# When the row additions, the expert work and the last chunk's row numbers are issued in a graph and expert layer

## The chip, the cores and the metric

The kernel runs on one core of a Trainium2 chip. The metric is the device time of one execution in microseconds. A time is the median of several runs; a profile comes from one execution. The engines are called PE (matrix), PEld (its weight loads), DVE (vector), ACT (scalar), POOL (general purpose, here only the sender of indirect transfers) and SP (here only a sender of transfers). Each takes its own instructions in their written order and waits on semaphores for the others.

## The reference, cut to what matters

There are 6250 nodes with 256 features and 100,000 edges, sorted by destination. The layer is a mean over neighbours with a linear map, and then a mixture of eight experts of which each node uses two:

```python
x = x + gnn(layernorm(x), edge_index)     # segment_sum(h[src], dst) / degree, then [h, agg] @ W.T + b
xn = layernorm(layernorm(x)) * gamma + beta
logits = xn @ Wr + br
top_vals, top_idx = top_k(logits, 2)
w = softmax(top_vals)
for e in range(8):
    h = gelu(xn @ W1[e] + b1[e])          # 256 -> 512
    y_e = h @ W2[e] + b2[e]               # 512 -> 256
    y = y + y_e * w_full[..., e, None]
out = x + y
```

All of it is computed in float32.

## The kernel before, in words

**Edges.** The 100,000 edges are padded to 784 *edge tiles* of 128. Fourteen tiles (`C`) make a *window*, and there are 56 windows (`W`). First the kernel forms `z_d`, the neighbour product of every node, and `u_d`, the node's own product. Then it takes one edge tile after another. `gather` (L553) is an indirect transfer on POOL of 128 rows of `z_d` into one of 28 buffers `xg` (`XG`), issued 28 tiles ahead of its use. `add_edges` (L570) multiplies these rows by a matrix of zeros and ones `hot` (made on DVE, L564), so that edges with one destination add up in the PSUM tile `pS`. When the 14 tiles of a window are through, `window_done` plans what follows: `shared_row` (L576, DVE) adds the row that two windows share, `keep_sums` (L580, ACT) copies the sums, `share_row` sends the row on to the next window by way of memory, and `window_x1` (L605 to L608) divides by the degree and adds the node's own product, which `load_u` (L597) has fetched. For the last window `load_u` is an indirect transfer on POOL (L599).

**Routing.** Four windows make a *chunk*, 14 in all. After a chunk's last window `window_done` plans the routing by counts of tiles: variances, roots, norms, the router's logits, the ranking (`route`), `exps`, `weigh`, `choices`, `count_tokens`, then for each of four windows `one_hot_slots` (L644, L645) and `sort_tokens` (L652 on PE, L655 on ACT), which sorts the tokens by expert into `xs`. `share_runs`, `place_rest`, `place_runs` and `tile_experts` work out on DVE where each run of tokens goes. `copy_runs` (L786, ACT) copies the runs of one expert into the slots `xe`, in eight calls of four copies each. `find_rows` (L756 on PE, L760 to L769 on DVE) gives each token the row number of its two results. `start_experts` releases the chunk's expert work. The class `Steps` holds the counts of tiles for the ordinary chunks and `LastSteps` those for the last chunk, whose routing comes behind the last edge.

**Expert work.** `expert_stages` gives 16 *tasks* for a chunk: eight `hidden` (L811 on PE, L816 Gelu on ACT) and eight `result` (L824 on PE; after every second one L828 on DVE adds the bias and L830 on SP stores 256 rows of `y`). The PSUM tile `py` has one buffer, so the next pair of results waits for L828. Chunks are joined in three *batches* of 6, 5 and 3 chunks. After a batch's last chunk `more_stages` does tiles of 128 tokens that overflowed their slots (7, 5 and 3 of them, three tasks each: L854, L858; L863, L866; L872, L876, L879).

**Additions.** When all expert work of a batch is planned, `sum_rows` starts the *additions*, one for each window: `gather_rows` loads the window's rows from `x1_d` (L908, SP) and its two result rows by two indirect transfers on POOL (L912), into the `xg` buffers that the edges no longer need. `add_rows` adds them with two L919 on DVE and `store` writes 128 rows of the output (L898, SP; the last window by an indirect transfer on POOL, L900). Additions start only where fewer than 28 edge tiles are left.

**What sets the order.** The order is written out by hand. The loop over edge tiles calls `after(t)` once for each tile `t`, and further with counts up to the end. `after` first issues what was planned with `at` for this `t`. Then it adds `pace` to an allowance, issues tasks from the list `tasks` until the allowance is spent, and calls `sum_rows`. `clock` is the planner's own estimate of time, by which an addition counts as due 10 us after its gather:

```python
        while adds and (adds[0][0] <= clock or not (sums or tasks)):
            adds.pop(0)[1]()
```

In this text *step* `t` is one call of `after`; the last edge tile is step 783.

Of the kernel before, what the change touches and what calls it, by code (L numbers as in the profile page):

```python
# [19 lines left out]
C = 14  # L20
TB = 4
UB = 2
CW = 4
# [7 lines left out]
def gnn_ffn_kernel(ctx: ExitStack, tc: tile.TileContext, x, x_cols, src, dst, dst_next, gw, gw_t, gb, gb_cols, gamma, beta,  # L31
# [39 lines left out]
    W = src.shape[1]  # L71
# [833 lines left out]
    def gather_rows(K, j, V):  # L905
        g = K.first + j
        V.o = spare()
        nc.sync.dma_start(V.o, x1_d[g * P:(g + 1) * P, :])  # L908
        G, i = K.group, j
        V.y2 = [spare() for _ in range(2)]  # L910
        for r in range(2):
            nc.gpsimd.indirect_dma_start(  # L912
                out=V.y2[r], out_offset=None, in_=K.batch.y[:, :],
                in_offset=bass.IndirectOffsetOnAxis(ap=G.rows[:, r, i:i + 1], axis=0))

    def add_rows(K, j, V):
        G, i = K.group, j
        for r in range(2):
            nc.vector.scalar_tensor_tensor(V.o, V.y2[r], G.w2[:, r, i:i + 1], V.o, op0=ALU.mult, op1=ALU.add)  # L919
        store(K, j, V.o)  # L920
# [4 lines left out]
    tasks, later, Ks, sums, adds = [], {}, [], [], []  # L925
    slots, w1_sb, w2_sb, xe = None, None, None, None
    now, spent, clock, due, spares = None, 0.0, 0.0, 0.0, 0
    class Steps:

        x1, var, roots, norms, route, exps, weigh, choices, count = 2, 5, 7, 9, 11, 14, 15, 16, 19  # L930
        hot, sort = (22, 24, 26, 28), (26, 28, 30, 32)
        runs, rest, place, tiles, copied, rows, pace, start = 30, 33, 36, 39, 40, 46, 1.5, 54

    class LastSteps:

        x1, var, roots, norms, route, exps, weigh, choices, count = 2, 4, 5, 6, 7, 8, 9, 10, 12
        hot, sort = (13, 14, 17, 18), (15, 16, 19, 20)
        runs, rest, place, tiles, copied, rows, pace, start = 15, 16, 19, 24, 21, 28, 1, 25

    def at(t, f, *args):  # L940
        later.setdefault(max(t, now), []).append(lambda: f(*args))
# [44 lines left out]
    def sum_rows():  # L986

        nonlocal due
        while adds and (adds[0][0] <= clock or not (sums or tasks)):
            adds.pop(0)[1]()  # L990
        left = W * C - 1 - now
        while sums and not sums[0][0].batch.left and clock >= due and left < XG:
            if 0 < left < XG and spares + 3 > XG - left:
                return
            K, j = sums.pop(0)
            V = Group()
            gather_rows(K, j, V)
            adds.append((clock + 10.0, lambda K=K, j=j, V=V: add_rows(K, j, V)))
            while len(adds) > XG // 3 - 1:
                adds.pop(0)[1]()  # L1000
            due = max(due, clock - 6.0) + (4.0 if left > 0 else 2.4)

    def after(t):
        nonlocal now, spent, clock
        now = t
        while later.get(t):
            later[t].pop(0)()
        later.pop(t, None)
        clock += 0.6 if t < W * C else 0.3 if tasks else 1.2

        pace = 0.72 if t < W * C else 1.2 if len(Ks) < W // CW else 2.0
        spent = min(spent + pace, pace) if tasks else 0.0
        while tasks and spent > 0:
            us, f, _ = tasks.pop(0)
            spent -= us
            clock += us
            f()
        sum_rows()
# [13 lines left out]
    for index in range(W // CW):  # L1032
# [10 lines left out]
        for g in range(K.first, K.first + CW):  # L1043
            if g > 0:
                V = V_next
            for c in range(C):
                t = g * C + c
                add_edges(V, c)
                if c == 0:
                    hot_tiles(V, HC)  # L1050
                if c == HC and g + 1 < W:
                    V_next = new_window(g + 1, V)
                if t + XG < len(edge_tiles):
                    gather(*edge_tiles[t + XG])
                for to, what in loads[:1]:
                    loads.pop(0)
                    nc.sync.dma_start(to, what)
                if u_tasks and t % 2 == 0:
                    u_tasks.pop(0)()
                    if not u_tasks:  # L1060
                        u_pools.close()
                        slots = fast_pools.enter_context(tc.tile_pool(name="slots", bufs=2))
                        xe = slots.tile([P, KD, SC], F32, name="xe", bufs=1)
                        for n in range(4):
                            at(t + 3 + 5 * n, clear_slots, n)
                        w1_sb, w2_sb, parts = weights(slots)
                        for n, (to, what) in enumerate(parts):
                            at(t + 2 + 2 * n, nc.scalar.dma_start, to, what)
                if c == HC + 5:
                    load_u(V)  # L1070
                if c == C - 1:
                    window_done(V, G, K, t)
                after(t)
    t = W * C
    while later or tasks or sums or adds:
        after(t)
        t += 1
# [149 lines left out]
```

## Time and profile before

| | |
|---|---|
| time, median of 3 runs | 1244.61 us (1242.8 to 1246.04) |
| profiled execution, its own time | 1243.91 us |
| its span, first to last instruction | 1242.0 us |
| PE busy | 1024.7 us (83%) |
| PEld busy | 870.2 us (70%) |
| DVE busy | 705.5 us (57%) |
| ACT busy | 454.6 us (37%) |
| POOL busy | 859.5 us (69%) |
| granted PE clock, mean | 0.924 of full |

The span is what the lines of the profile add up to; the execution's own time is 1.9 us longer, and the median of the runs is 0.7 us above that. Busy shares are means over very different stages: up to about 1055 us the edges run, and after it the last chunk is routed, its experts run, and nearly all the additions are made. POOL's busy time leaves out the pause of about 0.3 us between two of its indirect transfers, so that an engine that sends without a break shows as three quarters busy.

### The profile page before, as it was taken

What the parts mean: (1) busy time and instruction counts of PE and PEld (TensorE: products, weight loads), DVE (VectorE), ACT (ScalarE), POOL (GpSimd) and SP (SyncE); (2) the same over time, 40 slices, a digit from 0 to 9 for tenths busy, and PEclk for the clock granted to TensorE, in tenths of its full rate; (3) what the DMA queues carried; (4) which work ended last, traced back from release to release, by engine and by line L of the source; (5) the groups of instructions that cost most, each with busy time, mean ns of one, the idle gap of its engine ahead of it and who ended that gap; (6) DMA issues with size and microseconds to landing.
All of it is one profiled execution on the core that took longest, in us unless ns stands there. A gap on an engine that the chain in (4) does not pass through costs nothing. (4 is left out here: it accounts for less than half of the span.)

```text
span 1242.0 us, 18821 instructions
## 1 busy us (share of the span) xinstructions
PE 1024.7 (83%) x5236; PEld 870.2 (70%) x5236; DVE 705.5 (57%) x2436; ACT 454.6 (37%) x1264; POOL 859.5 (69%) x907
## 2 busy tenths in 40 slices
PE   7898837897979798897979999997979999675920
PEld 6676625786868687786857898886868788565710
DVE  5766657474646566464547556563655664483442
ACT  2400003534444344434443554435444544334200
POOL 0057777777777777777777777777777777775554
PEclk9999878898989899998999999998989999787965
DMA  9989895554555555454555555555555555665664
GB/s 335 359 277 310 251 368 151 137 154 137 156 142 148 152 144 155 136 160 130 154 141 161 140 154 153 153 153 144 148 146 151 151 154 149 198 197 165 192 182 131
DMA packets 139187, 221.02 MB, mean 178 GB/s; under 512 B 23108, under 2 KB 106255, under 8 KB 138950
## 3 DMA queue, kind: packets, MB, share of 16 engines
q0 software_dynamic: 43104, 120.94, 36.4%
q1 hardware_dynamic: 87638, 89.37, 21.7%
q10 hardware_dynamic: 8336, 9.45, 2.3%
q8 instruction: 44, 0.72, 0.2%
q14 instruction: 65, 0.53, 0.1%
HBM read 166.69 MB, written 53.02 MB: 177 GB/s over the span
## 5 line engine op out<-in xcount | busy, mean ns | idle before, releaser
L553 POOL DMA_INDIRECT xg<-z_d,src_i x784 | 747.7, 954 | 306.3 <-issue 115.5
L570 PE MATMUL pS<-xg,hot 128*128 128x265 f32 x1568 | 418.5, 398 | 20.1 <-issue 7.3
L570 PEld LDWEIGHTS pS<-xg,hot 128*128 128x128 f32 x1568 | 295.8, 196 | 78.7 <-issue 14.9
L811 PE MATMUL ph<-xe,w_sb 128*128 128x128 f32 x1792 | 237.3, 290 | 68.2 <-ACT xe L786 68.2
L811 PEld LDWEIGHTS ph<-xe,w_sb 128*128 128x128 f32 x1792 | 233.7, 205 | 79.5 <-ACT xe L786 73.1
L824 PE MATMUL py<-w_sb,hid 128*128 128x256 f32 x896 | 219.0, 390 | 13.5 <-DVE rows L828 13.5
L816 ACT ACTIVATE hid<-ph,b_sb 128x128 f32<-128x128 f32 x448 | 128.1, 369 | 243.5 <-PE ph L811 243.2
L824 PEld LDWEIGHTS py<-w_sb,hid 128*128 128x128 f32 x896 | 172.0, 195 | 42.4 <-ACT xe L786 13.0
L786 ACT ACTIVATE xe<-xs x448 | 139.3, 311 | 135.7 <-DVE rows L828 39.9
L912 POOL DMA_INDIRECT xg<-y_d,rows_i x112 | 108.5, 969 | 61.4 <-issue 19.8
L564 DVE TENSOR_TENSOR hot<-cols,rel 128x896 f32<-128x896 f32 x112 | 121.2, 1082 | 36.3 <-PE pS L570 33.1
L576 DVE TENSOR_TENSOR pS<-pS,row 1x265 f32<-1x265 f32 x55 | 23.5, 427 | 141.1 <-PE pS L570 130.1
L655 ACT ACTIVATE xs<-pm,beta_sb,gamma_sb 128x256 f32<-128x256 f32 x112 | 57.2, 560 | 75.5 <-PE pm L652 75.3
L828 DVE TENSOR_TENSOR rows<-py,b_sb 128x512 f32<-128x512 f32 x56 | 38.4, 685 | 79.7 <-PE py L824 77.1
L919 DVE SCALAR_TENSOR_TENSOR xg<-xg,w,xg 128x256 f32<-128x256 f32 x112 | 52.8, 483 | 37.6 <-DMA xg<-y_d,rows_i 34.9
L580 ACT ACTIVATE sums<-pS 128x265 f32<-128x265 f32 x56 | 21.7, 388 | 125.7 <-DVE pS L576 50.9
L255 PE MATMUL ph<-gc,x_t 128*128 128x264 f32 (+1 forms) x200 | 56.1, 404 | 11.8 <-DVE u_t L372 7.3
L652 PE MATMUL pm<-to,xn 128*128 128x256 f32 x224 | 57.6, 380 | 2.7 <-DVE to L645 2.7
L255 PEld LDWEIGHTS ph<-gc,x_t 128*128 128x128 f32 x200 | 37.4, 194 | 23.6 <-issue 7.1
L255 PE MATMUL pm<-gc,x_t 128*128 128x264 f32 (+1 forms) x192 | 53.1, 400 | 0.0
L816 ACT ACT_TABLE_LOAD x24 | 30.8, 1283 | 57.1 <-PE ph L811 56.9
L652 PEld LDWEIGHTS pm<-to,xn 128*128 128x128 f32 x224 | 42.4, 190 | 9.7 <-issue 3.0
(189 smaller groups left out, 817.9 us busy)
## 6 DMA issues: line engine op xcount, KB each, us to landing
y_d<-rows SPq DMA_DIRECT2D x56, 256.0 KB
xg<-z_d,src_i POOLq DMA_INDIRECT x784, 2.9
w_sb<-w_dram ACTq DMA_DIRECT2D x16, 512.0 KB
sums_d<-sums SPq DMA_DIRECT2D x55, 132.5 KB
x<-u_d SPq DMA_DIRECT2D x55, 132.0 KB
x_d<-x SPq DMA_DIRECT2D x56, 128.0 KB
xg<-x_d SPq DMA_DIRECT2D x56, 128.0 KB
out_dram<-xg SPq DMA_DIRECT2D x55, 128.0 KB
```

Source lines behind the costliest of these rows:

```text
L255: nc.tensor.matmul(pz, x_t[:, t, k, :], gc[:, h * KD + k, :n], start=(k == 0), stop=(k == KD - 1))
L553: nc.gpsimd.indirect_dma_start(out=xg[(g * C + c) % XG][:, :DZ], out_offset=None, in_=z_d[:, :], in_offset=bass.IndirectOffsetOnAxis(ap=sr ...
L564: nc.vector.tensor_tensor(hot, col[:, None, :].to_broadcast([P, HC, P]), V.rel[:, c:c + HC, None].to_broadcast([P, HC, P]), op=ALU.is_equal)
L570: nc.tensor.matmul(V.pS, V.hot[c // HC][:, c % HC, :], xg[(V.g * C + c) % XG], start=(c == 0), stop=(c == C - 1))
L652: nc.tensor.matmul(px[:, k, :], G.xn[i][:, k * P:(k + 1) * P], G.one_hot[i], start=True, stop=True)
L655: nc.scalar.activation(xs[:, at:at + 2 * P], px[:, k, :], AF.Identity, bias=beta_sb[:, k:k + 1], scale=gamma_sb[:, k:k + 1])
L786: nc.scalar.activation(xe[:, :, bass.ds(to_at, CAP)], src[:, :, bass.ds(src_at, CAP)], AF.Copy)
L811: nc.tensor.matmul(ph[:, i, a * SH:(a + 1) * SH], w1_sb[:, U.e + a, k, c * P:(c + 1) * P], xe[:, k, at:at + SH], start=(k == 0), stop=(k = ...
L816: nc.scalar.activation(U.hid[:, c, a * SH:(a + 1) * SH], ph[:, i, a * SH:(a + 1) * SH], AF.Gelu, bias=b1_sb[:, U.e + a, c:c + 1])
L824: nc.tensor.matmul(U.py[:, h, :], U.hid[:, c, h * P:(h + 1) * P], w2_sb[:, U.e + h, c, :], start=(c == 0), stop=(c == KH - 1))
L912: nc.gpsimd.indirect_dma_start(out=V.y2[r], out_offset=None, in_=K.batch.y[:, :], in_offset=bass.IndirectOffsetOnAxis(ap=G.rows[:, r, i:i ...
L919: nc.vector.scalar_tensor_tensor(V.o, V.y2[r], G.w2[:, r, i:i + 1], V.o, op0=ALU.mult, op1=ALU.add)
```

## The change

Four things change, all of them in when something is issued; no instruction is added or taken away.

- `start` of the ordinary chunks goes from 54 to 60 steps behind the chunk's last edge tile. The copies of a chunk are issued at steps 40 to 50.
- For the last chunk `rows` goes from 28 to 22 and `start` from 25 to 29. Its copies are issued at 21 to 28.
- `sum_rows` issues due additions only once the last edge tile has been issued. (Its second loop, which issues the oldest addition when nine are open, stays.)
- In the last 50 edge tiles `pace` is 0.4 in place of 0.72.

```diff
     class Steps:
 ...
-        runs, rest, place, tiles, copied, rows, pace, start = 30, 33, 36, 39, 40, 46, 1.5, 54
+        runs, rest, place, tiles, copied, rows, pace, start = 30, 33, 36, 39, 40, 46, 1.5, 60
 
     class LastSteps:
 ...
-        runs, rest, place, tiles, copied, rows, pace, start = 15, 16, 19, 24, 21, 28, 1, 25
+        runs, rest, place, tiles, copied, rows, pace, start = 15, 16, 19, 24, 21, 22, 1, 29
 ...
     def sum_rows():
 
         nonlocal due
-        while adds and (adds[0][0] <= clock or not (sums or tasks)):
+        while adds and now >= W * C and (adds[0][0] <= clock or not (sums or tasks)):
             adds.pop(0)[1]()
 ...
-        pace = 0.72 if t < W * C else 1.2 if len(Ks) < W // CW else 2.0
+        pace = 0.4 if W * C - 50 <= t < W * C else 0.72 if t < W * C else 1.2 if len(Ks) < W // CW else 2.0
```

## The prediction

> **What bounds the kernel now.** I read the costliest groups first, then the waits, then the timeline engine by engine from 1040 us on. The chain that ended last is of no use here: it goes back only to 1234 us. The waits of POOL (engine, line, who was waited for: total us, times, longest us):
>
> ```profile
> POOL xg L553 <- issue: 115.5, 379, 0.3
> POOL xg L553 <- PE pS L570: 71.0, 233, 0.3
> ```
>
> No edge gather waits longer than a pause of 0.3 us, whoever is named, after the one long wait at the start. From 149.2 to 1054.9 us POOL sends one every 1.2526 us (1054.90 - 1053.65 in the timeline). So the edge stage is as long as POOL's queue, and PE's 68.2 us of waiting for the copies (L811 on L786) cost nothing while edges run. The change can move only what lies behind 1056 us, some 186 us of 1242. The timeline there (start us, length us, engine, line; in brackets the idle time before and its releaser):
>
> ```profile
> 1054.90 0.95 POOL L553 DMA_INDIRECT xg<-z_d,src_i  x1 [0.30 <-issue]
> 1056.16 0.94 POOL L912 DMA_INDIRECT xg<-y_d,rows_i  x1 [0.30 <-issue]
> ...
> 1059.43 0.48 DVE L919 SCALAR_TENSOR_TENSOR xg<-xg,w,xg 128x256 f32<-128x256 f32 x1 [12.08 <-DMA xg<-y_d,rows_i]
> ...
> 1067.29 3.75 PE L824 MATMUL py<-w_sb,hid 128*128 128x256 f32 x8 [12.26 <-DVE rows L828]
> ...
> 1078.26 0.95 POOL L599 DMA_INDIRECT x<-u_d,tail_i  x1 [0.30 <-issue]
> ...
> 1079.35 5.52 PE L811 MATMUL ph<-xe,w_sb 128*128 128x128 f32 x48
> ...
> 1083.18 0.49 DVE L607 SCALAR_TENSOR_TENSOR x<-pS,rdeg,x 128x264 f32<-128x264 f32 x1
> ```
>
> The first addition is issued on DVE at step 766, but its result rows are sent by POOL only behind all edge gathers, at 1056.16. DVE stands from 1047.35 to 1059.43, L828 stands behind it, and PE stands 12.3 us with nine edge tiles still to do, all of whose rows are there by about 1058. The last edge ends at 1079.35, the last window's x1 comes at 1083.18. Further on:
>
> ```profile
> 1128.59 3.78 PE L811 MATMUL ph<-xe,w_sb 128*128 128x128 f32 x16 [5.88 <-ACT xe L786]
> 1134.83 3.38 PE L811 MATMUL ph<-xe,w_sb 128*128 128x128 f32 x16 [2.46 <-ACT xe L786]
> 1140.67 3.45 PE L811 MATMUL ph<-xe,w_sb 128*128 128x128 f32 x16 [2.46 <-ACT xe L786]
> ...
> 1146.58 2.61 PE L811 MATMUL ph<-xe,w_sb 128*128 128x128 f32 x16 [1.93 <-ACT xe L786]
> 1148.98 4.78 PE L824 MATMUL py<-w_sb,hid 128*128 128x256 f32 x16
> ...
> 1196.75 0.94 POOL L912 DMA_INDIRECT xg<-y_d,rows_i  x1 [10.45 <-DVE xg L919]
> ...
> 1225.65 7.21 SPq L898 DMA_DIRECT2D out_dram<-xg  x4
> 1226.04 0.95 POOL L912 DMA_INDIRECT xg<-y_d,rows_i  x1 [0.30 <-issue]
> ...
> 1235.16 1.02 POOL L900 DMA_INDIRECT out_dram<-xg,tail_i  x1 [8.18 <-SPq L1086]
> ```
>
> The last chunk's first four hidden tasks each wait for a copy, since the chunk is started at step 808 with copies up to 811, and ACT takes copy and Gelu in turn: they fill 1128.59 to 1148.98, 20.4 us. PE's last result is DVE's L876 at 1191.39; its y rows leave SP at 1193.87 behind other work, and POOL starts the last batch's 24 row gathers at 1196.75 (the releaser named is not the cause: the rows' landing is). These take 30.2 us, and SP's output stores, 2.29 us apart in the last four, end 5 us behind the additions. The last store waits for them.
>
> **What the Trainium skill says.** "PSUM — Partial Sum Buffer", section "Engine vs sequencer instructions": the queues of ACT, DVE and POOL are strict FIFO. The trace agrees: L828 and L576 stand behind L919. "TensorE: Matmul & The Clock Gate", section on the HAM clock gate: PE idle for a window of about 3.4 us falls to half rate. The trace agrees: after 12.26 us idle eight L824 took 3.75 us against 1.89 elsewhere. "ScalarE: Activation LUTs", "What ACT_TABLE_LOAD costs": 1283 ns a load, and the trace has 1283.
>
> **The change part by part.** *Start 60.* 16 tasks at 0.72 a step still end before the next chunk's half of `xe` is needed; it takes PE's waits for copies away where POOL hides them. Worth 0; the cover is the ring of 28 gathers, 35 us long, and PE was 5 tiles (6 us) late at 1055. If the cover went, each us would count.
>
> *Pace 0.4.* 50 x 0.32 = 16 units of allowance less, and 6 x 0.72 = 4.3 by the later start, at about 1.9 a task: some 11 tasks fewer before the last edge. The planner followed by hand says the same: behind the last edge stand 9 tasks of chunk 11 and all 16 of chunk 12, where before 14 of chunk 12 stood. A task is 1.76 us (x16 L811 every 1.78, x8 L824 every 1.73), so 19.4 us of PE work moves behind the edges. What hides it: PE's idle time from 1081 to 1191 us, 27.5 us summed from the timeline's brackets, and 9 us lost at low clock. Cover gone, it costs 19.4.
>
> *Additions behind the last edge.* PE keeps up with the gathers: last edge about 1059.5 instead of 1079.4. But that gain does not pass on whole. The last window's own row (L599) is sent by POOL behind 16 row gathers: 1056.16 + 16 x 1.2526 = 1076.2, and a gather lands 3.2 us after its start (1226.04 to 1229.20), so x1 comes at 1079.4, only 3.8 us earlier. Six additions are issued at once ahead of it on DVE; the last rows for them start at 1069.9 and land at 1073.1, so they are done first. L828 behind x1 holds `py`: PE does five tasks and stands from 1068 to 1082.
>
> From x1 I add DVE's pieces as they stand in the timeline, additions (0.95 each) where they are now issued: x1 and statistics 1.2, addition 1.0, variances and L828 0.7 (1082.4); the root no longer waits 2.9 us behind Gelus; norms and logits 2.85, addition, route 2.36, weigh 0.8, addition, choices 1.0 (1091.3); L828, addition, count 1.6, addition, one-hot 1.0, then a wait of 2.1 for two results at half clock as at 1104.94 before (1098.5); L828, addition, one-hot, runs 1.5, addition, rest 3.1, one-hot, addition, one-hot, addition, place 1.85: 1112.1 against 1118.3. Copies start at 1113 instead of 1119.5, 6.5 us earlier.
>
> *Start 29.* PE fills the copies' 8 x 1.76 us with the last thirteen tasks of chunk 12; ACT does two groups of Gelus between the copies and is through with them at 1129, and my walk through both queues ends the thirteen tasks at 1135. Chunk 13 then runs without waits: four hidden tasks to 1142.2 where before they ended at 1149.0. Gain 6.8 us. From there the same 12 tasks and overflow tiles follow (1149.0 to 1191.4 before), so the last L876 is at 1184.6; at best 4 us less, since one overflow copy (L858) waited 4.19 us for an SP store that should now be through, at worst nothing less. Taking half: 1182.6; L876 and its store 0.5, landing 2.9 (1193.87 to 1196.75), so POOL starts its last 24 at 1186.0.
>
> *Rows 22.* L756 and eleven DVE instructions (2.3 us) move from behind a 15.87 us DVE wait to before it: 0, hidden by DVE's idle time.
>
> *End.* All 44 earlier additions are now issued before the last y store, so SP has only the last batch's stores left: they keep POOL's 2.505 us a window. Last addition 32.9 us after POOL starts, as before; the final store is released 0.6 us later instead of 4.7, and 7.7 us remain (1234.34 to 1242). End = 1186.0 + 33.5 + 7.7 = 1227.2. Against the span 1242.0 that is -14.8. The execution's time is 1.9 above the span, the median 0.7 above that: 1230.
>
> POOL bounds the gain: 113 transfers from 1056.16 take 141.5 us, to 1197.7, and 15 follow (1227 to 1242): a span of 1213 at least.
>
> **The rivals.** *Little passes on* (0.14): the last window's row by POOL fixes x1, PE's stall is only moved, DVE stays the chain; then x1's 3.8 us and part of SP's 4 remain, time 1237 to 1241. For it: L599's place. Against it: the four hidden tasks' 20.4 us, which depend on start 29. *The moved work bounds* (0.06, slower): 11 tasks, 19.4 us, on PE behind the edges. My walk leaves PE some 16 us of waits and low clock after 1082; if it loses the 36 us of before, the time is 1250, and from 15 us above my walk on the kernel is slower. Against it: there is now other work to fill the waits. *Output stores on SP bound* (0.04, slower): each waits for the one before, and the y rows of the last results stand behind 28 stores from 1115 on. At 2.47 us (mean from 1195 to 1232) they leave at 1184, a little late; from 2.95 us on the kernel is slower, at 3.2 us the time is 1251. *More* (0.05): overflow waits vanish and PE stays at full clock, 1216 to 1222. *Nothing* (0.04): the stall is refilled elsewhere in full, within 0.3%.
>
> **How the numbers follow.** My own case has 0.67, 1223 to 1237, the spread being the 4 us of the overflow copies, the 2 us of each result pair at low clock, and some us in my walk. With part of "more" and "little" the range 1220 to 1241 holds 0.8. A difference under 0.3% (3.7 us) is about what a measurement of this kernel cannot tell from none. Faster: 0.67 + 0.05 + 0.14 = 0.86; same 0.04; slower 0.06 + 0.04 = 0.10.
>
> **What would show it.** Right: no PE wait for L828 around 1055 to 1067; last L570 near 1060; L599 near 1076 and x1 near 1079.5; no L811 wait for L786 above 1 us after 1080; first last-batch row gather near 1186; stores at the end in step with POOL. Wrong: an edge gather that waits over 0.3 us, PE idle 15 us or more between 1082 and 1180, the last y store held behind a queue of L898, or the last batch's gathers starting after 1197.

## The result, and the profile after

The median is 1234.81 us (1234.78 to 1235.89 in four runs) where the kernel before, run beside it, has 1244.46 us (1242.8 to 1246.04 in four): a ratio of 0.9925, with a 95% interval of 0.9907 to 0.9942. The change saves 9.7 us. Forecast were 14.6, so the direction and the range hold and a third of the gain is missing. The profiled execution took 1235.89 us, its span is 1234.1 us against 1242.0 before.

The stall in the last edges is gone. From the timeline of the kernel after (start us, length us, engine, line; in brackets the idle time before and its releaser):

```profile
1052.42 0.95 POOL L553 DMA_INDIRECT xg<-z_d,src_i  x1 [0.31 <-PE pS L570]
...
1057.42 2.27 PE L570 MATMUL pS<-xg,hot 128*128 128x265 f32 x4 [2.86 <-DMA xg<-z_d,src_i]
1060.08 2.36 DVE L919 SCALAR_TENSOR_TENSOR xg<-xg,w,xg 128x256 f32<-128x256 f32 x5
...
1073.90 0.95 POOL L599 DMA_INDIRECT x<-u_d,tail_i  x1 [0.30 <-issue]
...
1077.22 0.49 DVE L607 SCALAR_TENSOR_TENSOR x<-pS,rdeg,x 128x264 f32<-128x264 f32 x1 [5.81 <-DMA x<-u_d,tail_i]
...
1080.02 5.79 PE L824 MATMUL py<-w_sb,hid 128*128 128x256 f32 x16 [9.50 <-DVE rows L828]
```

PE ends the last edge tile at 1059.7, with nothing but a gather's landing to wait for, and the additions start behind it. DVE then waits 5.81 us for the last window's own row from L599. A PE stall of 9.50 us remains, moved behind the edges: L828 stands behind x1. The last chunk's copies start at 1110.11 where before they started at 1119.5. From there on:

```profile
1133.14 7.31 PE L811 MATMUL ph<-xe,w_sb 128*128 128x128 f32 x64
1140.28 3.62 PE L824 MATMUL py<-w_sb,hid 128*128 128x256 f32 x16
...
1149.72 3.72 PE L824 MATMUL py<-w_sb,hid 128*128 128x256 f32 x16 [2.25 <-DVE rows L828]
...
1158.01 3.72 PE L824 MATMUL py<-w_sb,hid 128*128 128x256 f32 x16 [1.00 <-DVE rows L828]
...
1166.66 1.03 DVE L919 SCALAR_TENSOR_TENSOR xg<-xg,w,xg 128x256 f32<-128x256 f32 x2 [1.33 <-DMA xg<-x_d]
1167.61 0.68 DVE L828 TENSOR_TENSOR rows<-py,b_sb 128x512 f32<-128x512 f32 x1
1168.44 5.93 PE L824 MATMUL py<-w_sb,hid 128*128 128x256 f32 x16 [6.71 <-DVE rows L828]
1174.21 3.60 PE L854 MATMUL ph<-w_sb,xe 128*128 x8
...
1189.24 0.43 DVE L876 TENSOR_TENSOR rows<-py,b_sb 128x256 f32<-128x256 f32 x1 [2.15 <-PE py L872]
...
1193.38 0.94 POOL L912 DMA_INDIRECT xg<-y_d,rows_i  x1 [20.46 <-DMA xg<-x_d]
```

The first four hidden tasks of the last chunk run as one piece of 7.31 us, without a wait for a copy; before they took from 1128.59 to 1148.98 with four such waits. The gain at this point is 8.7 us (1148.98 - 1140.28). Of these, 2.5 us lie in the edge stage of the two profiles: POOL sends the last edge gather at 1052.42 here and at 1054.90 before. Counted from that gather, the gain is 6.2 us. Then three waits of PE for L828, 2.25, 1.00 and 6.71 us, take it away: L854 comes at 1174.21, 2.0 us *later* than the 1172.21 of before. DVE's waits between 1080 and 1193 us name what it stood for (engine, line, who was waited for: total us, times, longest us). After:

```profile
DVE xg L919 <- DMA xg<-x_d: 20.8, 11, 3.1
```

and in the same stretch of the kernel before:

```profile
DVE xg L919 <- DMA xg<-x_d: 0.9, 1, 0.9
```

It is not the two result rows from POOL that the additions wait for, but the third row, which L908 loads from `x1_d` by SP. In SP's queue each L908 is issued behind output stores (L898), and these are slow. SP's own waits from 1061 to 1193 us, after:

```profile
SPq L898 <- DMA out_dram<-xg: 49.1, 36, 4.1
SPq L898 <- DVE xg L919: 8.9, 6, 6.2
```

and a piece of its timeline there:

```profile
1160.59 0.34 SPq L898 DMA_DIRECT2D out_dram<-xg  x1
1161.03 0.38 SPq L908 DMA_DIRECT2D xg<-x_d  x1
1162.94 0.34 SPq L898 DMA_DIRECT2D out_dram<-xg  x1
...
1180.24 7.87 SPq L898 DMA_DIRECT2D out_dram<-xg  x4
1188.20 2.95 SPq L879 DMA_DIRECT2D y_d<-rows  x3
```

Of the 44 stores up to 1193 us, 36 wait for the store before them to land, and only six for their own addition. (Before, in the same stretch, 27 waited so, 37.4 us in all.) The wait is an instruction of the program: the trace has an EVENT_SEMAPHORE on SP ahead of each of the 55 stores of the kernel, 17 to 4104 ns long. From 1147.15 to 1167.83 nine stores are issued, one per 2.58 us. The loads come in the gaps, so the additions go at the stores' pace. So the chain reads: store on SP, L908 behind it, L919 for that row, L828 behind L919 on DVE, the next pair of results on PE. At 1180.24 four stores in a row even hold back the last batch's y rows (L879).

The table gives the stages of the tail in the profiles of five kernels, of which three are experiments told below (us; "pairs" is the time from the end of the four hidden tasks to the first L854; "additions ahead" are those that stand in DVE's order ahead of the first of the last chunk's four L828):

| | last edge gather | four hidden done | pairs | last L876 | first last-batch gather | span | additions ahead |
|---|---|---|---|---|---|---|---|
| before | 1054.90 | 1148.98 | 23.2 | 1191.39 | 1196.75 | 1242.0 | 25 |
| after | 1052.42 | 1140.28 | 33.9 | 1189.24 | 1193.38 | 1234.1 | 31 |
| gate alone | 1054.61 | 1144.58 | 22.1 | 1188.45 | 1192.28 | 1238.3 | 25 |
| pace 0.72 | 1054.36 | 1138.27 | 22.1 | 1180.71 | 1188.23 | 1228.6 | 28 |
| additions 3.0 apart | 1053.06 | 1139.60 | 22.1 | 1177.18 | 1181.27 | 1229.8 | 27 |

A span is one execution's and is no substitute for a median. The profile of after is of the slowest of its four runs (1235.89 us, median 1234.81), that of the last row of the fastest of its six (1231.58, median 1233.97). Where a few us count, the stages are better counted from the last edge gather.

### The profile page after: what moved, and what is told of

It reads as the page before. It is cut to its first block, busy times and chain, and to the rows that moved or that the text cites. A ratio compares the mean times of both kernels' runs of the same rounds, so it can differ in the third digit from the quotient of the medians.

```text
span 1234.1 us, 18849 instructions
## 1 busy us (share of the span) xinstructions
PE 1050.9 (85%) x5236; PEld 859.5 (70%) x5236; DVE 704.4 (57%) x2436; ACT 457.6 (37%) x1265; POOL 857.2 (69%) x907
## 3 DMA queue, kind: packets, MB, share of 16 engines
q1 hardware_dynamic: 87638, 89.37, 22.1%
## 5 line engine op out<-in xcount | busy, mean ns | idle before, releaser
L570 PE MATMUL pS<-xg,hot 128*128 128x265 f32 x1568 | 458.9, 417 | 75.6 <-DMA xg<-z_d,src_i 53.5
L570 PEld LDWEIGHTS pS<-xg,hot 128*128 128x128 f32 x1568 | 292.5, 201 | 177.1 <-DMA xg<-z_d,src_i 91.7
L824 PE MATMUL py<-w_sb,hid 128*128 128x256 f32 x896 | 217.8, 389 | 21.3 <-DVE rows L828 21.2
L811 PEld LDWEIGHTS ph<-xe,w_sb 128*128 128x128 f32 x1792 | 224.3, 198 | 8.3 <-ACT xe L786 1.0
L811 PE MATMUL ph<-xe,w_sb 128*128 128x128 f32 x1792 | 226.3, 282 | 0.7 <-ACT hid L816 0.5
L824 PEld LDWEIGHTS py<-w_sb,hid 128*128 128x128 f32 x896 | 173.2, 195 | 51.7 <-DVE rows L828 13.3
L786 ACT ACTIVATE xe<-xs x448 | 139.4, 311 | 102.3 <-ACT xe L786 33.9
L564 DVE TENSOR_TENSOR hot<-cols,rel 128x896 f32<-128x896 f32 x112 | 121.1, 1082 | 89.8 <-PE pS L570 88.2
L828 DVE TENSOR_TENSOR rows<-py,b_sb 128x512 f32<-128x512 f32 x56 | 38.6, 689 | 114.2 <-PE py L824 114.2
L919 DVE SCALAR_TENSOR_TENSOR xg<-xg,w,xg 128x256 f32<-128x256 f32 x112 | 53.3, 482 | 55.9 <-DMA xg<-y_d,rows_i 33.5
```

Source lines behind the costliest of these rows:

```text
L564: nc.vector.tensor_tensor(hot, col[:, None, :].to_broadcast([P, HC, P]), V.rel[:, c:c + HC, None].to_broadcast([P, HC, P]), op=ALU.is_equal)
L570: nc.tensor.matmul(V.pS, V.hot[c // HC][:, c % HC, :], xg[(V.g * C + c) % XG], start=(c == 0), stop=(c == C - 1))
L786: nc.scalar.activation(xe[:, :, bass.ds(to_at, CAP)], src[:, :, bass.ds(src_at, CAP)], AF.Copy)
L811: nc.tensor.matmul(ph[:, i, a * SH:(a + 1) * SH], w1_sb[:, U.e + a, k, c * P:(c + 1) * P], xe[:, k, at:at + SH], start=(k == 0), stop=(k = ...
L824: nc.tensor.matmul(U.py[:, h, :], U.hid[:, c, h * P:(h + 1) * P], w2_sb[:, U.e + h, c, :], start=(c == 0), stop=(c == KH - 1))
```

## The experiments

The first is one edit of the kernel before, the others are one to three edits of the changed kernel; "gate" means the condition `now >= W * C` in `sum_rows`. The kernels of one group ran on one chip beside the kernel before, whose medians were 1244.70, 1242.84 and 1243.03 us in the three groups. Since the groups are of different chips, ratios to the kernel before are compared; the changed kernel's is 0.9925. Each ratio stands with its 95% interval. From these intervals (0.0010 to 0.0021 either way; 0.0018 for the changed kernel) I estimate that a difference of two ratios under about 0.0025, 3 us, is not resolved.

**First group: what each part is worth.**

The gate alone, on the kernel before:

```diff
-        while adds and (adds[0][0] <= clock or not (sums or tasks)):
+        while adds and now >= W * C and (adds[0][0] <= clock or not (sums or tasks)):
```

> The kernel before with one edit: additions only behind the last edge tile. Theory A (the last window's row, sent by POOL behind 16 row gathers, fixes x1 once DVE's stall is gone): PE's 12.3 us wait for L828 near 1055 vanishes, the last edge tile ends near 1060 instead of 1079, but x1 (last L607) comes only some 4 us earlier, and the copies and Gelus in turn at the end stay; time 1238 to 1242, that is 3 to 6 us less than before. Theory B (the stall was the whole loss): the end moves with the last edge, time 1229 or less.

1240.47 us, 0.9969 (0.9959 to 0.9979): 3.9 us. The stall's 12.3 us on PE become 3.4 us of x1 (1079.81 against 1083.18), because L599 keeps its place behind the result rows, and 4.4 us at the end of the hidden tasks. The last edge ends at 1070.6 and not near 1060 as expected: without the stall PE still ends 16 us behind the last edge gather, but x1 waits for L599 and not for it. The hidden tasks still wait for the copies, as before; PE's waits from 1050 to 1200 us:

```profile
PE ph L811 <- ACT xe L786: 13.3, 5, 6.2
```

The change without the gate:

```diff
-        while adds and now >= W * C and (adds[0][0] <= clock or not (sums or tasks)):
+        while adds and (adds[0][0] <= clock or not (sums or tasks)):
```

> The changed kernel with the condition on additions taken out again; 5 additions are then issued before step 784. Theory A: DVE stands some 12 us for the first row gather, PE behind it, x1 comes 2 to 6 us later than in the changed kernel and the end with it: 1236 to 1241. Theory C (the gain is all in the pace and the later start): the time stays at 1235 within 1 us.

1239.61 us, 0.9957 (0.9943 to 0.9971): by the ratios the gate is worth some 4 us in this company too. The profile shows less of it. x1 (1080.85) is 3.6 us later than in the changed kernel, but 3.2 of these are a later last edge gather (1055.58), and counted from it the span is 1.4 us longer. The old stall is back, here ahead of the edges' own `hot` on DVE. The waits from 1050 to 1200 us:

```profile
DVE xg L919 <- DMA xg<-y_d,rows_i: 26.4, 5, 22.2
...
PE pS L570 <- DVE hot L564: 10.9, 1, 10.9
```

The change with the old pace:

```diff
-        pace = 0.4 if W * C - 50 <= t < W * C else 0.72 if t < W * C else ...
+        pace = 0.72 if t < W * C else ...
```

> The changed kernel with the pace of 0.72 kept through the last 50 edge tiles; no task of chunk 11 is then left behind the last edge (9 in the changed kernel). Theory A (behind the edges PE works without a break from 1095 to 1149, and x1 hangs on POOL and not on the edges): 9 tasks of 1.76 us less in that stretch, the last chunk's first hidden task starts up to 12 us earlier than at 1133; of this the SP queue leaves 3 to 8: time 1227 to 1232. Theory D (less expert work beside the last edges is what helps): edges end late, x1 comes later than 1078, time 1236 to 1244.

1230.35 us, 0.9893 (0.9878 to 0.9908): *faster* than the change, by some 4 us; the two intervals just touch. Two further kernels with the old pace, told below, have 0.9880 and 0.9884, with intervals clear of the changed kernel's. So pace 0.4 doesn't help, it costs. The timeline of PE says how:

```profile
1128.82 9.61 PE L811 MATMUL ph<-xe,w_sb 128*128 128x128 f32 x64 [5.07 <-ACT xe L786]
1138.27 3.62 PE L824 MATMUL py<-w_sb,hid 128*128 128x256 f32 x16
...
1160.34 3.60 PE L854 MATMUL ph<-w_sb,xe 128*128 x8
```

The 19.4 us of tasks that pace 0.4 moves behind the edges are paid directly with only about 2 us at the end of the hidden tasks (1140.28 - 1138.27; 4.0 counted from the last edge gather), although here the wait for a copy is back. The larger part, 11.8 us, lies in the pairs of results, 22.1 us in place of 33.9. Here 28 additions go ahead of them and not 31. At the stores' 2.58 us three more additions are, by my estimate, 7.7 us; the three PE waits above add up to 10.0. Some of this is given back before the end: the last batch's gathers start 7.5 us behind L876 (4.1 in the changed kernel), since SP issues its third L879 only at 1183.74, behind a store (1183.36) that stood for the one before it.

The change with the last chunk's old counts:

```diff
-        runs, rest, place, tiles, copied, rows, pace, start = 15, 16, 19, 24, 21, 22, 1, 29
+        runs, rest, place, tiles, copied, rows, pace, start = 15, 16, 19, 24, 21, 28, 1, 25
```

> The changed kernel with rows 28 and start 25 for the last chunk, as before. Theory A as predicted (start 29 keeps copies and Gelus from going in turn): the last chunk's first four hidden tasks wait for copies again and the time rises by 5 to 9 us to 1240 to 1244. Theory E (25 tasks are left behind the edges, so the last chunk's tasks come up only behind the copies whatever start says): the last chunk's first hidden task is issued one step earlier than in the changed kernel, no wait for copies above 1 us, time 1235 within 1 us.

1238.89 us, 0.9958 (0.9943 to 0.9974). No L811 waits for a copy, although the chunk is released at step 808 while its copies go on to 811: with pace 0.4, 25 tasks are left behind the edges, all ahead of the chunk's own in PE's order, and its first hidden task comes at step 817. So it is not start 29 that removed the copy waits in the changed kernel, but the moved work. This is theory E's forecast for the waits; its forecast for the time fails, since by the ratios the kernel is some 4 us above the changed one. The profile doesn't show where they lie. Counted from the last edge gather (1054.73) the hidden tasks end 0.8 us earlier than in the changed kernel, the last L876 comes 1.1 us later, and the span is 0.5 us shorter. What differs is that the overflow tiles take 18.9 us (1173.74 to 1192.68) in place of 15.0, with one wait for a y store:

```profile
1181.66 2.73 PE L854 MATMUL ph<-w_sb,xe 128*128 x4 [3.88 <-DVE rows L858]
```

Why that store is late, and whether the row numbers' place or the start counts here, was not tested.

**Second group: is the edge stage touched, and which wait counts?**

Ordinary chunks' start back to 54:

```diff
-        runs, rest, place, tiles, copied, rows, pace, start = 30, 33, 36, 39, 40, 46, 1.5, 60
+        runs, rest, place, tiles, copied, rows, pace, start = 30, 33, 36, 39, 40, 46, 1.5, 54
```

> The changed kernel with start 54 for the ordinary chunks, as before. Theory A (edges are bound by POOL, so PE's waits for copies there are free): the edge gathers end at the same time; two tasks less stand behind the last edge, 3.5 us of PE work, so the time is 0 to 3 us lower, 1232 to 1235. Theory F (the waits for copies cost time): PE falls behind, edge gathers wait over 0.3 us or the last edge comes later, time 1238 or more.

1236.44 us, 0.9948 (0.9935 to 0.9961). PE waits 63.9 us for copies while the edges run, and still no edge gather waits over 0.3 us, as forecast for a stage that is POOL's alone; the last one is sent at 1056.04. The time isn't lower, as the first reading had it. By the ratios start 60 is worth some 3 us here, with intervals that overlap: not resolved.

The load of `x1_d` on ACT's queue in place of SP's:

```diff
-        nc.sync.dma_start(V.o, x1_d[g * P:(g + 1) * P, :])
+        nc.scalar.dma_start(V.o, x1_d[g * P:(g + 1) * P, :])
```

> The changed kernel with the loads of the windows' rows (L908) sent from ACT's queue in place of SP's. Theory A (the rows' loads stand on SP behind output stores that follow each other at 2.3 us and more, DVE's additions wait for the loads, L828 behind the additions, PE behind L828): L919's wait for these loads falls from 20.8 us to under 4, PE's waits for L828 between 1140 and 1175 from some 11 us to under 3, the last batch's gathers start 5 to 9 us earlier than at 1193, time 1226 to 1230. Theory G (the stores themselves hold the end, since the last y rows stand behind all 44 of them): the wait moves to the y rows, time 1232 to 1236.

1239.07 us, 0.9973 (0.9961 to 0.9984), *slower* than the change by some 6 us, which no expectation gave. The wait that was meant goes, from 20.8 to 6.0 us, and with it the long pairs: with 31 additions ahead, as in the changed kernel, they take 22.9 us in place of 33.9. So it is the loads behind the stores that held the pairs up, and not the number of additions by itself. But the stores are as serial as before. The waits from 1050 to 1200 us:

```profile
DVE rows L858 <- DMA y_d<-rows: 6.6, 1, 6.6
DVE xg L919 <- DMA xg<-x_d: 6.0, 4, 2.0
```

and SP's timeline:

```profile
1144.67 12.79 SPq L898 DMA_DIRECT2D out_dram<-xg  x6
1157.52 0.43 SPq L830 DMA_DIRECT2D y_d<-rows  x1
...
1189.26 5.47 SPq L879 DMA_DIRECT2D y_d<-rows  x3
```

Freed from the loads, the additions run ahead and their stores pile up in front of the y rows on SP: a y store waits behind six stores, L858 waits for a row buffer that such a y store holds, and PE waits 4.5 us for Gelus on ACT, where the loads now are. The four hidden tasks end at 1147.93, 5.1 us later than in the changed kernel counted from the last edge gather. It looks as if the loads in SP's queue had been a brake that kept the additions in step with the stores; this was not tested by itself.

The last window's own row sent ahead of the result rows:

```diff
-                if c == HC + 5:
+                if c == (HC + 5 if g < W - 1 else 0):
                     load_u(V)
```

> The changed kernel with the last window's own row fetched at its first edge tile, so that POOL sends it ahead of 8 of the 16 row gathers. Theory A (this row fixes x1): L599 some 10 us earlier, x1 at 1072 to 1073 instead of 1077, now behind the six additions on DVE; the routing moves with it, time lower by 2 to 5 us. Theory G (output stores hold the end): x1 earlier, end unchanged within 1 us.

1234.89 us, 0.9930 (0.9913 to 0.9947). x1 comes without a wait:

```profile
1075.84 0.49 DVE L607 SCALAR_TENSOR_TENSOR x<-pS,rdeg,x 128x264 f32<-128x264 f32 x1
```

Counted from the last edge gather (1055.84 here) that is 20.0 us, against 24.8 in the changed kernel. By the ratio nothing of the 4.8 us reaches the time, as theory G has it. In the profile part of it stays: L919 waits 23.3 us for `x_d`, 2.5 more than in the changed kernel, and the last L876 (1189.66) is, counted in the same way, 3.0 us earlier. The two don't agree, and why is open; in this kernel an earlier x1 is worth nothing that the times show.

Both edits together:

> The row loads on ACT's queue and the last window's own row early, together. Theory A: the gains add, 8 to 12 us below the changed kernel, 1223 to 1227. Theory G: 1232 or more.

1237.57 us, 0.9957 (0.9944 to 0.9970). The expected sum isn't there: the time is 2.7 us above that with the early row alone and 1.5 us below that with the loads on ACT alone.

**Third group: additions in step with the stores.**

Additions of the tail planned 3.0 units apart in place of 2.4:

```diff
-            due = max(due, clock - 6.0) + (4.0 if left > 0 else 2.4)
+            due = max(due, clock - 6.0) + (4.0 if left > 0 else 3.0)
```

> The changed kernel with additions behind the last edge tile spaced by 3.0 in place of 2.4 on the planner's clock. Ahead of the last chunk's four result pairs stand then 27, 30, 33 and 34 additions in place of 31, 35, 39 and 40 (25, 29, 32, 34 in the kernel before), and 37 in place of 44 ahead of the last y store. Theory A (the additions are issued faster than SP can store, 2.3 us and more apart, and L828 stands behind them): L919's waits for the windows' rows fall from 20.8 us to under 8, PE's waits for L828 between 1140 and 1175 to under 3, the last L876 comes 6 to 9 us earlier; 4 to 5 us are given back at the end, where seven more stores are left: 1229 to 1233. Theory G (the sum of the stores holds the end): as many stores at the same pace, 1234 to 1237.

1233.97 us, 0.9924 (0.9910 to 0.9939). The waits behave as theory A has it: with 27 additions ahead of the last chunk's pairs, L919 waits 7.8 us for the windows' rows between 1080 and 1193 us, and the pairs run through in 22.1 us. From the timeline:

```profile
1161.68 3.60 PE L854 MATMUL ph<-w_sb,xe 128*128 x8
...
1181.27 1.21 POOL L912 DMA_INDIRECT xg<-y_d,rows_i  x1 [6.86 <-DVE xg L919]
...
1222.98 1.02 POOL L900 DMA_INDIRECT out_dram<-xg,tail_i  x1 [10.94 <-SPq L1086]
```

L876 and the last batch's gathers come 12 us earlier than in the changed kernel. And yet the time is the same within the interval, so the forecast of 1229 to 1233 isn't met: 37 additions go ahead of the last y store in place of 44, so seven more stores are left for the end. POOL is through with its gathers, and its last store L900 then waits 10.9 us for SP to be through with the stores before it (4.0 in the changed kernel; L1086 is what SP does behind them). What DVE doesn't wait for is waited for at the end.

Old pace, and start 25 for the last chunk:

```diff
-        runs, rest, place, tiles, copied, rows, pace, start = 15, 16, 19, 24, 21, 22, 1, 29
+        runs, rest, place, tiles, copied, rows, pace, start = 15, 16, 19, 24, 21, 22, 1, 25
```

> The changed kernel with pace 0.72 throughout and start 25 for the last chunk, rows left at 22. Few tasks are left then, and the last chunk's first hidden task is issued one copy before the end of the copies. Theory A: one turn of copy and Gelu comes back, 1 to 3 us over the same kernel with start 29 (1230.35): 1231 to 1234. Theory H (start 29 is worth the whole 13 us by which the four first hidden tasks took too long): 1240 or more.

1229.23 us, 0.9880 (0.9859 to 0.9901), against 0.9893 with start 29. The loss of 1 to 3 us isn't there. PE waits twice for copies, 3.25 and 2.46 us, and has the four hidden tasks done at 1139.18, 0.9 us later (2.1 counted from the last edge gather); start 29 is worth nothing that shows in the time.

Old pace, and the own row early:

> The changed kernel with pace 0.72 throughout and the last window's own row fetched at its first edge tile. Theory A: in this kernel the routing of the last window is what PE and ACT wait for (PE idle 16 us before 1083, 5 us for copies), so the 3 us by which x1 was late for its row pass on: 1226 to 1229. Theory G (stores hold the end): 1230 within 1 us.

1228.49 us, 0.9884 (0.9866 to 0.9903): within the uncertainty of the old pace alone. L876 (1179.69) and the first last-batch gather (1186.93) are 1.0 and 1.3 us earlier by the clock, and at the same place within 0.3 us counted from the last edge gather. As in the changed kernel, the earlier row gains nothing that shows.

Old pace, own row early, additions 3.0 apart:

> Pace 0.72 throughout, the last window's own row early, and additions spaced by 3.0. Theory A: with PE ahead, fewer additions before the last y rows leave more stores for the end than they save: 1226 to 1231. Theory G: 1230 or more.

1232.49 us, 0.9916 (0.9900 to 0.9931), some 4 us slower than without the wider spacing, with intervals that just overlap. L876 is at 1172.60, the earliest of all, and the stores are further behind than ever: L900 waits 15.2 us for them.

The three kernels with the gate and the old pace and additions 2.4 apart, at 0.9880 to 0.9893, are the fastest here and beat both kernels of this case.

**What the gain is made of.** The gate alone is worth 3.9 us and pace 0.4 costs some 4. So the larger part of the 9.7 us comes from the rest, start 60, start 29 and rows 22: on one chip the gate alone has 1240.47 us, and with these three beside it, at the old pace, the kernel has 1230.35, 10.1 us less. Start 29 is worth nothing there. Start 60 and rows 22 are left, and no run takes these two apart. What the profiles show with both and without start 29 (0.9880), against the gate alone: PE is 5.9 us behind the last edge gather at the end of the edges and not 16.0, the last chunk's hidden tasks wait twice for copies, 5.7 us, and not four times, 13.0 us, DVE's wait of 14.8 us for L756 is down to 0.2, and 42 additions in place of 39 go ahead of the last y store, so that fewer stores are left for the end.

## Why the prediction was right, and where it was wrong

By its own steps, against the trace (us):

| step | foretold | measured |
|---|---|---|
| last edge ends | 1059.5 | 1059.7 |
| L599 sent | 1076.2 | 1073.90 |
| x1 | 1079.4 | 1077.22 |
| PE's stall behind x1 ends | 1082 | 1080.02 |
| copies start | 1113 | 1110.11 |
| thirteen tasks of chunk 12 done | 1135 | 1133.14 |
| four hidden tasks done | 1142.2 | 1140.28 |
| last L876 | 1182.6 | 1189.24 |
| first last-batch gather | 1186.0 | 1193.38 |
| span | 1227.2 | 1234.1 |

**Up to 1140 us the walk was right.** From L599 on every step is 2 to 3 us early, and most of that offset is the edge stage's: the last edge gather is sent at 1052.42 in this execution, at 1054.90 in that of before, and between 1052.4 and 1056.0 over the executions profiled here, of different kernels and on several chips. L599 is 2.3 us early for this reason. That the gain on PE doesn't pass on whole because L599 stands behind the result rows (a rival by its own) was right in size: x1 came 24.8 us behind the last edge gather where before it came 28.3, 3.5 us less.

**The step that failed is "From there the same 12 tasks and overflow tiles follow".** The four hidden tasks before them ran without waits, as foretold. I gave the rest 40.4 us, from the hidden tasks to the last L876; it took 49.0. The twelve tasks account for it: 33.9 us in place of the 23.2 of before (the overflow tiles behind them took 15.0 us in place of 19.2, so that the "at best 4 us less" came in full). The additions' third row and its place on SP were not in my walk: in the trace of before the wait for it is 0.9 us in all, and I took that as its price, where it was the price with 25 additions ahead and not with 31. Pace 0.72 and the wider spacing both bring these twelve tasks back to 22.1 us, and both leave fewer additions ahead; with the loads taken off SP's queue they take 22.9 us with all 31 ahead. That is the evidence. The serial stores were in the prediction, as a rival with 0.04 and with 2.47 us each, but I looked for them only in front of the last y rows, and on the slower side. They hold there too (L879 behind four L898 at 1180.24, POOL's start 4.1 us behind L876 where I had 3.4), but that is 0.7 us. Two of the signs of being wrong that I had named did show: PE's waits between 1082 and 1180 us add up to 19 us, more than the 15 named, and the last y store stood behind a queue of L898.

**Start 29 had no part in it.** That the first four hidden tasks ran without waits I had put down to it. But as the last chunk's old counts show, the waits go with pace 0.4 and start 25 too, and at the old pace start 29 changes nothing that shows in the time. The effect was right, the reason wrong.

**Two terms put at nothing were not nothing.** Start 60 and rows 22 ("Worth 0" and "0, hidden by DVE's idle time") go together with most of the 10.1 us above; which of the two, and by what path, stays open. That the time still came out near is owed to the walk, which followed the queues of the whole changed kernel up to 1140 us; what I said of the worth of its single parts holds only for the gate (3.9 us measured, 3.8 foretold for x1).

**"Hidden by PE's idle time" was half right.** Of the 19.4 us moved by pace 0.4, 2 to 4 show at the end of the hidden tasks. What I had not asked is what else the moved tasks shift: the planner lets additions come due while tasks are issued, so a longer backlog puts more additions ahead of the last pairs: 25 with 14 tasks behind the last edge, 28 with 16, 31 with 25. The net cost is some 4 us of the time.

**The end was right.** From POOL's start 40.7 us were left (1234.1 - 1193.38) against 41.2 foretold, with the stores in step. The additive sum was off by 8.6 us in one term, the offset of 1.9 us at 1140 went the other way, and the median, which had been reckoned 2.6 us above the span, lies 0.7 us above it: 14.6 foretold, 9.7 measured.

**Order and clock.** What I took from the Trainium skill agrees with the trace of after too. "PSUM — Partial Sum Buffer", section "Engine vs sequencer instructions", has DVE's queue as a strict FIFO, and it is this order that carries the wait for one row over to L828 and PE. "TensorE: Matmul & The Clock Gate", in its section on the HAM clock gate, says that PE falls to half rate after an idle window of about 3.4 us, and that shows again: behind the 9.50 us stall sixteen L824 took 5.79 us, behind the 6.71 us one 5.93 us, where they take 3.62 in stretches without a stall. So these two stalls cost 2.2 and 2.3 us more than their own length.

## What to carry to other kernels

A wait that reads as nothing in the profile before has its price only at the rate of before: where a change issues work faster, go through every transfer that this work needs, queue by queue, and compare the new rate with what stands ahead of it there. Work that a planner paces by its own clock moves whenever other work moves, so count what comes ahead of the last critical task after a change, not only what was moved. Where stores go one after another, issuing them in a different rhythm can merely choose who waits: additions early held up PE here, additions late held up the end. And a part of a change that is put at nothing deserves a run of its own: here two such parts went together with the larger share of the gain.

## What the runs showed of the hardware that was not expected

- Output stores (L898, 128 KB each) go one at a time: 36 of the 44 up to 1193 us wait for the landing of the one before, and they are one per 2.58 us in the busy stretch. Everything that stands behind them in SP's order, loads and y rows alike, waits with them; six in a row took 12.79 us in the kernel with the loads on ACT. SP doesn't wait like this behind every transfer: it issues seven loads (L908) in 4.19 us at 1191.25. The wait is the semaphore wait of the program ahead of each store, whose place in `out` is read at run time (`window_rows`). What the stores would do without it was not tested.
- The edge stage, 784 indirect transfers in POOL's queue, sent its last gather between 1052.42 and 1056.04 us in the profiles here, and behind the one long wait at the start no gather waits over 0.3 us in any of them. The profiles are of different kernels on several chips; the four of the third group, on one chip, lie between 1053.06 and 1053.50, those of the second, on another, between 1052.68 and 1056.04. A profile's later steps carry this offset, about the size of the smallest effects sought here.
